# Triangle product and gated pair layer: four edits around the start and the end of the first stage

## The chip, the cores and the metric

The kernel runs on one core of one Trainium2 chip. The metric is the device time of one execution in microseconds (us). Three executions of the kernel before took 3205.04, 3205.08 and 3206.83 us; the median is 3205.08 us.

## What is computed

The input `x` is 384 x 384 positions of 128 channels in float32. Two layers follow each other.

```
z_n = layernorm(x)
a   = (z_n Wa + ba) * sigmoid(z_n Wga + bga)
b   = (z_n Wb + bb) * sigmoid(z_n Wgb + bgb)
t   = einsum('ijd,jkd->ikd', a, b)             # for each channel d one 384x384x384 product
x1  = x + (layernorm(t) Wo + bo) * sigmoid(z_n Wgo + bgo)

left  = x1 W_left + x1 W_eq + biases,  right = x1 W_right + b_right
out   = (left * sum_j right) * sigmoid(x1 W_gate + b_gate)
y     = layernorm(out W_out + b_out + x1)
```

## The kernel before

The work has three stages, and all of the change lies in the first and at its border to the second.

**Stage 1, projections.** The positions are cut into 72 tiles `n` (128 rows by 16 columns, `NT = 72`), and each tile into four steps `s = 4n + t` of four columns. A step (`step`, line 284) makes four products of 128x512 on TensorE (`proj` for `ga`, `a`, `gb`, `b`, line 305), two sigmoids on ScalarE (line 313), and on VectorE the two products `at` (line 326) and `bt` (line 342). `gate_project` (line 261) makes the eight small products `pgo` of the output gate (line 268) and adds their bias on VectorE into `gs` (line 270); `gate` (line 251) takes the sigmoid of `gs` on ScalarE into the tile `gt` (line 255), and after the fourth step of a tile stores `gt` to the DRAM tensor `G` from the GpSimd queue (line 258).

For tiles 0 to 2 `x` is normalised on ScalarE (line 222) and turned by TensorE. From tile 3 on (`OLD = 3`) a turned copy of `x` is loaded as `zT`. Its rows have to be multiplied by a factor per position: GpSimd makes the factors (`turned_factors`, lines 178 to 184, the last one a power), ScalarE copies them sixteen times into `again` (`repeat`, line 192, in the second step of the tile before), and `normalise_turned(s)` (line 196) multiplies. It is called in step `s - 2`. VectorE spreads the factors of two columns into the SBUF tile `every` and of the other two into the PSUM tile `pevery` (both line 210), and then GpSimd multiplies the first half and VectorE the second (both line 214). GpSimd also adds a bias to every tile for the residual (`residual`, line 233) and issues the stores of `Z` (234), `A` (330) and `G` (258).

The statistics of `x` (`bn_stats`, line 157, and `bn_aggr`, line 159) run on VectorE at the head of each step for columns that come some steps later. In step 0 they are those of the first four columns of tile 1, and the four GpSimd instructions of `norm_factors(1, 0, 4)` (lines 167 to 170) follow them.

The last 16 steps (`s >= S2 = 272`, tiles 68 to 71, the last group of 64 columns) leave out `gate_project`. Their 64 `pgo` products are made after the last step, in a row, "late gates": `gs`, sigmoid, store. `gt` comes from a pool of two buffers (`p1g`), `zT` from one of four (`p1z`), `gs` from one of three; the products of the projections share six PSUM banks.

**Stage 2, one 384x384x384 product per channel.** `fetch(d)` (line 640) loads the two factors of the `d`-th channel in the order of work, `ab_d`, from the DRAM tensors `A` and `B`, on SyncE's queue. Eight pairs are held. The pairs lie where pools of stage 1 lay: channels 0 to 3 mostly over a buffer of `bt`, channels 4 and 5 over buffers of `xt`. Channels under `BY_THIRDS = 2` are loaded by thirds of the rows of the sum: first two thirds (`fetch(d, 0, NB - 1)`), later the last third (`fetch(d, NB - 1)`), each third of `B` by a DMA of its own in pieces of 64 numbers (256 bytes). The other channels are loaded whole, in pieces of 768 bytes of `B`. The last rows and columns of `B` are still in SBUF (`b_held`) when stage 1 ends; `store_held` (line 661) stores them in pieces of some channels, of which the first covers channels 0 to 7. `multiply` (line 674) makes the products `pm` (line 679) in five PSUM banks: for `EARLY`, five (channel, row block) pairs of channels 0 and 1, first over two thirds, so that they don't need the last rows. `product` (line 685) ends them. VectorE subtracts channel 0 (`xd`, line 692), ScalarE squares (697), GpSimd adds (699), SyncE stores `X` (700).

**Stage 3** normalises, makes the second layer and stores; the change does not touch it.

The order on each engine is the order of the program. On SyncE's queue each DMA also waits until the one eight places before it has landed.

Of the kernel before, what the change touches and what calls it, by code (L numbers as in the profile page):

```python
# [9 lines left out]
FP = mybir.dt.float32  # L10
AF = mybir.ActivationFunctionType
ALU = mybir.AluOpType
# [8 lines left out]
def kernel(ctx: ExitStack, tc: tile.TileContext, ins, out: bass.AP):  # L21
# [15 lines left out]
    nc = tc.nc  # L37
    ctx.enter_context(tc.manual_schedule())
    P = 128
    x, xT = ins["x"][0], ins["xT"]  # L40
    N, C = x.shape[1], x.shape[2]
# [60 lines left out]
    CX, CT, BR = 16, 4, 32  # L102
    TS, TG = CX // CT, CG // CX
    OLD, SQ = 3, 32
    NT = NB * (N // CX)
    S2 = (NT - TG) * TS
# [4 lines left out]
    with tc.tile_pool(name="wprep", bufs=6) as wp, tc.tile_pool(name="p1s", bufs=3) as ps, tc.tile_pool(  # L111
        name="p1g", bufs=2
    ) as pgt, tc.tile_pool(name="p1z", bufs=4) as pz, tc.tile_pool(name="p1a", bufs=2) as pa_, tc.tile_pool(
        name="p1x", bufs=3
    ) as px, tc.tile_pool(name="p1b", bufs=1, side="right") as pb_, tc.tile_pool(name="p1t", bufs=2, space=PSUM) as ppt, tc.tile_pool(
        name="p1p", bufs=6, space=PSUM
    ) as ppp:
        tiles, turned, bts, gated, b_out_of = {}, {}, {}, {}, []
# [5 lines left out]
        def fetch(n):  # L124
            for _ in fetch_parts(n, 1):
                pass
# [27 lines left out]
        def statistics(first, last):  # L154
            for k in range(first, min(last, NT * CX)):
                n, c = divmod(k, CX)
                nc.vector.bn_stats(tiles[n]["st"][:, c, :], tiles[n]["x"][:, c, :])
                if n < OLD:
                    nc.vector.bn_aggr(tiles[n]["mv"][:, c, :], tiles[n]["st"][:, c, :])

        def norm_factors(n, c0=0, c1=CX, beside=nc.gpsimd):
            if n >= NT:
                return
            if n >= OLD:
                return turned_factors(n, c0, c1)
            mv, rstd, off = (tiles[n][k][:, c0:c1] for k in ("mv", "rstd", "off"))
            beside.tensor_scalar(rstd, mv[:, :, 1], EPS, None, ALU.add)
            beside.tensor_scalar(off, mv[:, :, 0], -1.0, None, ALU.mult)
            nc.gpsimd.tensor_tensor(rstd, rstd, mhalf[:, 0 : c1 - c0], ALU.pow)
            nc.gpsimd.tensor_tensor(off, off, rstd, ALU.mult)  # L170
            if c0 == 0:
                tiles[n]["zT"] = pz.tile([P, CX, C], FP, tag="zT", name=f"zn_{n}")
# [23 lines left out]
        def normalise_turned(s):  # L196
            n, t = divmod(s, TS)
            if n >= NT:
                return
            z = tiles[n]["zT"][:, t * CT : (t + 1) * CT, :]  # L200
            H = CT // 2
            for k, engine in enumerate((nc.gpsimd, nc.vector)):

                if k == 0:
                    every = ps.tile([P, H, P], FP, tag="every", name=f"every_{s}")
                else:
                    every = ppt.tile([P, CT, P], FP, tag="ptr", name=f"pevery_{s}")[:, 0:H, :]
                half = slice(k * H, (k + 1) * H)
                blocks = tiles[n]["again"][:, t * CT : (t + 1) * CT, :][:, half, :].rearrange("p c b -> p (c b)")
                nc.vector.transpose(  # L210
                    every.rearrange("p c (b r) -> p (c b) r", r=SQ),
                    blocks[:, :, None].to_broadcast([P, H * P // SQ, SQ]),
                )
                engine.tensor_tensor(z[:, half, :], every, z[:, half, :], ALU.mult)  # L214
            turned[s] = z

        def normalise(n, t, cs=range(CT)):
# [43 lines left out]
        def gate_project(s):  # L261
            n, t = divmod(s, TS)
            if t == 0:
                tiles[n]["gt"] = pgt.tile([P, CX, C], FP, tag="gt", name=f"gt_{n}")
            zT = turned[s]
            pgo = ppp.tile([P, CT, C], FP, tag="pk", name=f"pgo_{s}")
            for c in range(CT):
                nc.tensor.matmul(pgo[:, c, :], lhsT=zT[:, c, :], rhs=wT["go"], start=True, stop=True)  # L268
            gs = ps.tile([P, CT, C], FP, tag="gs", name=f"gs_{s}")
            nc.vector.tensor_tensor(gs, pgo, over(gate_bias, CT), ALU.add)  # L270
            gated[s] = gs
# [3 lines left out]
        FIRST_FACTORS = {  # L275
            0: ((1, 0, 4),), 1: ((1, 4, 8),), 2: ((1, 8, 12),), 3: ((1, 12, 16),),
            4: ((2, 0, 4),), 5: ((2, 4, 12),), 6: ((2, 12, 16),), 7: ((3, 0, 8),), 9: ((3, 8, 16),),
        }
        FIRST_RESIDUALS, FIRST_FETCHES = {2: 0, 5: 1, 9: 2, 10: 3}, {2: 3, 5: 4, 9: 5}

        def columns_ahead(s):
            return CX + CT * s + 2 * min(max(s - TS, 0), 2 * TS)

        def step(s):
            n, t = divmod(s, TS)
            r0, c0 = place(n)
            if t == 0:
                if n >= OLD:
                    fetch(n + 3)
                fetch_turned(n + 2)  # L290
                if s >= CATCH_UP:
                    norm_factors(n + 1)
                tiles[n]["at"] = pa_.tile([P, CX, P], FP, tag="at", name=f"at_{n}")
                if c0 % CG == 0:
                    bts[n // TG] = (pb_ if (NT - 1 - n) // TG % 2 else pb_held).tile(
                        [P, P, CG], FP, tag="bt", name=f"bt_{n}"
                    )
            at, bt = tiles[n]["at"], bts[n // TG]
            k0 = c0 % CG + t * CT
            zT = turned[s]  # L300
            ahead = (n + 1, t - 1) if t else (n, TS - 1)

            def proj(k):
                pk = ppp.tile([P, CT, P], FP, tag="pk", name=f"p{k}_{s}")
                nc.tensor.matmul(pk, lhsT=wT[k], rhs=zT, start=True, stop=True)  # L305
                return pk

            def by_rows(p):
                return p.rearrange("d c r -> d r c")

            def sigmoid(k, pg, by_row=False):
                sg = ps.tile([P, P, CT] if by_row else [P, CT, P], FP, tag="sg", name=f"sg{k}_{s}")
                nc.scalar.activation(sg, by_rows(pg) if by_row else pg, AF.Sigmoid, bias=bcol["g" + k])  # L313
                return sg

            statistics(columns_ahead(s), columns_ahead(s + 1))
            for factors in FIRST_FACTORS.get(s, ()):
                norm_factors(*factors)
            pga, pa = proj("ga"), proj("a")
            if s == 0:  # L320
                nc.tensor.matmul(biases[:, 1, :], lhsT=nb_w, rhs=raw["go"], start=True, stop=True)
                nc.vector.tensor_tensor(gate_bias, biases[:, 1, :], gate_bias, ALU.add)
            sga = sigmoid("a", pga)
            if 0 < s <= S2:
                gate(s - 1)
            nc.vector.scalar_tensor_tensor(
                at[:, t * CT : (t + 1) * CT, :], pa, bcol["a"], sga, ALU.add, ALU.mult
            )
            if t == TS - 1:
                nc.gpsimd.dma_start(out=A[:, c0 : c0 + CX, r0 : r0 + P], in_=at)  # L330
            pgb = proj("gb")
            sgb = sigmoid("b", pgb, by_row=True)
            if t == 1 and n + 1 >= OLD:
                repeat(n + 1)
            if s + 1 < OLD * TS:
                turn(s + 1)
                turned_out(s + 1)
            if s == 0:
                normalise(0, 2)
            normalise(*ahead)  # L340
            pb = proj("b")
            nc.vector.scalar_tensor_tensor(
                bt[:, :, k0 : k0 + CT], by_rows(pb), bcol["b"], sgb, ALU.add, ALU.mult
            )
            if s < S2:
                gate_project(s)
            if s + 2 >= OLD * TS:
                normalise_turned(s + 2)
            if s < CATCH_UP:
                if s in FIRST_RESIDUALS:  # L350
                    residual(FIRST_RESIDUALS[s])
                if s in FIRST_FETCHES:
                    fetch(FIRST_FETCHES[s])
            elif t == 1:
                residual(n + 1)
            if k0 + CT == CG and n < NT - 1:
                b_out_of.extend((bt, r0, c0 + CX - CG, k) for k in range(0, P, BR))
            if t == TS - 1 and b_out_of:
                bt, r0, k0, r = b_out_of.pop(0)
                nc.sync.dma_start(out=B[:, k0 // CG, r0 + r : r0 + r + BR, :], in_=bt[:, r : r + BR, :])  # L360
# [118 lines left out]
    x0, s1, s2, rs0 = (acc[:, k] for k in range(4))  # L479
    nc.gpsimd.memset(s1, 0.0)  # L480
    nc.gpsimd.memset(s2, 0.0)
    LAST, AHEAD, BY_THIRDS, R, HELD = 8, 6, 2, 4, 16
    group = {}

    def load(u):
# [135 lines left out]
    with tc.tile_pool(name="p2", bufs=1, side="right", reuse_waits="tile") as p2, tc.tile_pool(  # L621
        name="p2s", bufs=12, side="right", reuse_waits="tile"
    ) as p2s, tc.tile_pool(name="p2p", bufs=5, space=PSUM, reuse_waits="tile") as pp2, tc.tile_pool(
        name="p2q", bufs=2, space=PSUM, reuse_waits="tile"
    ) as pq2, tc.tile_pool(name="p2t", bufs=1, space=PSUM, reuse_waits="tile") as pt2:
        factors, products, squares = {}, {}, []
# [80 lines left out]
        for d in range(BY_THIRDS):  # L707
            fetch(d, NB - 1)
        store_held()
        for d in range(BY_THIRDS, AHEAD):  # L710
            fetch(d)
        store_held()
        for d, ib in EARLY:
            multiply(d, ib, range(NB - 1))
# [33 lines left out]
    with tc.tile_pool(name="p3s", bufs=4, reuse_waits="tile") as ps, tc.tile_pool(  # L748
        name="p3g", bufs=4, reuse_waits="tile"
    ) as pg3, tc.tile_pool(name="p3f", bufs=2, space=PSUM, reuse_waits="tile") as pfp, tc.tile_pool(  # L750
        name="p3y", bufs=2, space=PSUM, reuse_waits="tile"
# [294 lines left out]
```

## Time and profile before

| | |
|---|---|
| median of three executions | 3205.08 us |
| the profiled execution | 3205.72 us |
| its span, first to last instruction | 3203.9 us |
| TensorE busy | 3168.4 us, 99% |
| VectorE busy | 2703.2 us, 84% |
| GpSimd busy | 2414.4 us, 75% |
| ScalarE busy | 2009.0 us, 63% |
| stage 1 | 0 to 1283 us |
| stage 2 | 1283 to about 2045 us |

In the profile PE is TensorE, PEld its weight loads, DVE VectorE, ACT ScalarE, POOL GpSimd, SP SyncE. A row of the timeline gives the start in us from the span's start, the length, the engine, the line, what is written from what, and, in square brackets, how long the engine stood idle before it and what ended that.

### The profile page before, as it was taken

The page shows a single profiled execution, that of the slowest core. Times are in us where ns is not written, and L with a number is a line of the kernel's source. Part 1 is how long each engine was busy: PE and PEld are TensorE (multiplying, and loading weights), DVE is VectorE, ACT ScalarE, POOL GpSimd, SP SyncE. Part 2 cuts the span into 40 slices and gives each one's busy share as a digit, 9 for nine tenths or more (in the row PEclk, how much of TensorE's full clock was granted, in tenths as well). Part 3 has the DMA queues.
Part 4 walks back from the last instruction along what each step waited for, and adds up shares of the span by engine and source line. Part 5 has one row for each costly group of instructions (what it writes and reads, how often), then busy time and mean ns, then how long its engine had stood idle before and what let it go on. Part 6 is the DMA issues. An engine that isn't in the chain of part 4 may idle for free.

```text
span 3203.9 us, 51462 instructions
## 1 busy us (share of the span) xinstructions
PE 3168.4 (99%) x14543; PEld 2086.5 (65%) x14543; DVE 2703.2 (84%) x8313; ACT 2009.0 (63%) x5225; POOL 2414.4 (75%) x2113
## 2 busy tenths in 40 slices
PE   8999999999999999999999999999999999999998
PEld 5555555555555555555555555788888888888886
DVE  6999999999999997455555555999999999999999
ACT  7566666666666665222222222588888888888888
POOL 6788888888888876455555555499999998888888
PEclk9999999999999999999999999999999999999999
DMA  6989999999999998999999999777777777777774
GB/s 211 367 338 362 370 371 366 360 365 350 373 370 363 369 364 287 373 317 312 311 315 309 311 310 291 248 273 255 262 273 257 261 273 254 265 264 260 265 266 158
DMA packets 419195, 982.76 MB, mean 307 GB/s; under 512 B 30288, under 2 KB 326352, under 8 KB 373728
## 3 DMA queue, kind: packets, MB, share of 16 engines
q1 hardware_dynamic: 377984, 752.64, 67.5%
q0 software_dynamic: 40352, 226.57, 18.0%
q8 instruction: 118, 1.93, 0.2%
q14 instruction: 165, 1.35, 0.1%
q10 hardware_dynamic: 576, 0.26, 0.0%
HBM read 526.39 MB, written 452.98 MB: 306 GB/s over the span
## 4 chain that ended last, share of the span: by engine, by line
PE 95%; DMA 2%; POOL 1%; ACT 1%; issue 1%; DVE 1%; SPq 0%; ACTq 0%; POOLq 0%; DVEq 0%
PE pm L679 23%; PE py L519 8%; PE pf L789 8%; PE pleft L815 8%; PE pg L817 8%; PE pgo L268 7%; PE pga L305 7%; PE pa L305 7%; PE pgb L305 7%; PE pb L305 7%; PE ptr L542 4%; DMA B<-bt 1%; PE pg L828 0%; POOL acc L233 0%; DMA xt<-in_x_dram 0%
## 5 line engine op out<-in xcount | busy, mean ns | idle before, releaser
L679 PE MATMUL pm<-ab 128*128 128x384 f32 x2304 | 744.2, 486 | 2.0 <-DVE gs L270 2.0
L699 POOL TENSOR_TENSOR acc<-acc,xd 128x384 f32<-128x384 f32 x381 | 379.9, 997 | 361.9 <-DVE xd L692 361.8
L679 PEld LDWEIGHTS pm<-ab 128*128 128x128 f32 x2304 | 437.2, 190 | 306.4 <-DVE gs L270 2.6
L697 ACT ACTIVATE sq<-xd 128x384 f32<-128x384 f32 x381 | 188.4, 495 | 541.4 <-DVE xd L692 541.2
L692 DVE TENSOR_TENSOR xd<-pm,acc 128x384 f32<-128x384 f32 x381 | 212.3, 557 | 342.3 <-POOL acc L699 314.6
L807 ACT ACTIVATE res<-res,off,rs 128x128 f32<-128x128 f32 x1134 | 474.8, 485 | 0.4
L525 DVE SCALAR_TENSOR_TENSOR py<-py,acc,gr 128x128 f32<-128x128 f32 x1152 | 452.9, 393 | 0.9 <-PE py L519 0.2
L313 ACT ACTIVATE sga<-pga,c_L_conv_bga 128x512 f32<-128x512 f32 x288 | 197.9, 687 | 347.3 <-PE pga L305 345.6
L530 DVE BATCH_NORM_STATS2 st<-res 128x6 f32<-128x128 f32 x1128 | 375.3, 333 | 0.0
L268 PEld LDWEIGHTS pgo<-wT_go,xT 128*128 128x128 f32 x2208 | 287.5, 192 | 124.8 <-issue 78.4
L840 POOL TENSOR_TENSOR res<-res,r_L_conv_ln_bias 128x1536 f32<-128x1536 f32 (+1 forms) x96 | 326.5, 3401 | 7.5
L839 POOL TENSOR_TENSOR res<-res,r_L_conv_ln_scale 128x1536 f32<-128x1536 f32 (+1 forms) x96 | 326.9, 3406 | 0.6 <-ACT res L807 0.5
L233 POOL TENSOR_TENSOR acc<-xt,r_L_conv_b_out 128x2048 f32<-128x2048 f32 x72 | 327.0, 4541 | 0.0
L519 PE MATMUL py<-w_o,xr 128*128 128x128 f32 x2304 | 320.0, 275 | 0.0
L822 ACT ACTIVATE sg<-pg,c_L_conv_b_gate 128x384 f32<-128x384 f32 x384 | 223.2, 581 | 152.5 <-PE pg L817 103.6
L789 PE MATMUL pf<-w_o,h 128*128 128x128 f32 x2280 | 316.7, 275 | 0.0
L214 POOL TENSOR_TENSOR xT<-every,xT 128x256 f32<-128x256 f32 x276 | 202.0, 732 | 150.1 <-DVE every L210 144.4
L815 PE MATMUL pleft<-pairT,m_L_conv_W_left 128*128 128x384 f32 x768 | 311.6, 487 | 0.4 <-ACT pairT L543 0.4
L817 PE MATMUL pg<-pairT,m_L_conv_W_gate 128*128 128x384 f32 x768 | 310.6, 486 | 0.0
L305 PE MATMUL pga<-xT,wT_ga 128*128 128x512 f32 x552 | 284.1, 596 | 6.7 <-POOL xT L214 6.5
L519 PEld LDWEIGHTS py<-w_o,xr 128*128 128x128 f32 x2304 | 288.3, 192 | 0.8
L268 PE MATMUL pgo<-wT_go,xT 128*128 128x128 f32 x2208 | 288.5, 275 | 0.0
(187 smaller groups left out, 6667.6 us busy)
## 6 DMA issues: line engine op xcount, KB each, us to landing
Z<-acc POOLq DMA_DIRECT2D x72, 1024.0 KB, 10.5
A<-at POOLq DMA_DIRECT2D x72, 1024.0 KB, 13.4
G<-gt POOLq DMA_DIRECT2D x72, 1024.0 KB, 10.8
gr<-G SPq DMA_DIRECT2D x96, 768.0 KB, 5.7
zr<-Z SPq DMA_DIRECT2D x96, 768.0 KB, 7.2
xr<-X SPq DMA_DIRECT2D x96, 768.0 KB, 8.2
X<-xd SPq DMA_DIRECT2D x381, 192.0 KB, 5.6
xt<-in_x_dram SPq DMA_DIRECT2D x71, 1024.0 KB, 7.3
```

Source lines behind the costliest of these rows:

```text
L233: nc.gpsimd.tensor_tensor(zb, tiles[n]["x"], over(b_out, CX), ALU.add)
L268: nc.tensor.matmul(pgo[:, c, :], lhsT=zT[:, c, :], rhs=wT["go"], start=True, stop=True)
L305: nc.tensor.matmul(pk, lhsT=wT[k], rhs=zT, start=True, stop=True)
L519: nc.tensor.matmul(py[:, q, :], lhsT=g["x"][:, i, q * P : (q + 1) * P], rhs=w_o0, start=True, stop=True)
L525: nc.vector.scalar_tensor_tensor(py[:, q, :], py[:, q, :], rs0[:, q, u : u + 1], g["g"][:, i, q, :], ALU.mult, ALU.mult)
L530: nc.vector.bn_stats(b["st"][:, k, q, :], b["res"][:, k, q, :])
L679: nc.tensor.matmul(products[d, ib].rearrange("p (s c) -> p s c", c=CG), lhsT=ab[:, 0, q, ib * P : (ib + 1) * P], rhs=b_of(d)[:, :, q, :], ...
L699: nc.gpsimd.tensor_tensor(s1[:, ib, :], s1[:, ib, :], xd, ALU.add)
L789: nc.tensor.matmul(pf[:, q, :], lhsT=h[:, q * P : (q + 1) * P], rhs=w_o, start=True, stop=True)
L807: nc.scalar.activation(g["res"][:, i, q, :], g["res"][:, i, q, :], AF.Identity, bias=g["off"][:, i, q : q + 1], scale=g["rs"][:, i, q : q ...
L815: nc.tensor.matmul(pleft, lhsT=w_left, rhs=pairT, start=True, stop=True)
L817: nc.tensor.matmul(pg[:, 0:N], lhsT=w_gate, rhs=pairT, start=True, stop=True)
```

## The change

Four edits, with no change to the arithmetic:

1. For the last 16 steps `normalise_turned` makes one spread of 128x512 into PSUM and one product of 128x512, both on VectorE, in place of two spreads of 128x256, one product on GpSimd and one on VectorE.
2. For the same steps `gt` is not a tile of its own: the sigmoid of the late gates is written over the `zT` it was made from, and the store to `G` reads that.
3. In step 0 the statistics of tile 1 and the factors from them come after `gate_project`, not at the head of the step.
4. `BY_THIRDS` goes from 2 to 6: channels 2 to 5 are loaded by thirds as well, their first two thirds before the first `store_held` and their last third before the second one.

```diff
-            H = CT // 2
-            for k, engine in enumerate((nc.gpsimd, nc.vector)):
-                if k == 0:
+            H = CT // 2 if s < S2 else 0
+            for engine, k0, k1 in ((nc.gpsimd, 0, H), (nc.vector, H, CT)):
+                if k0 == k1:
+                    continue
+                if k0 < H:
                     every = ps.tile([P, H, P], FP, tag="every", name=f"every_{s}")
                 else:
-                    every = ppt.tile([P, CT, P], FP, tag="ptr", name=f"pevery_{s}")[:, 0:H, :]
+                    every = ppt.tile([P, CT, P], FP, tag="ptr", name=f"pevery_{s}")[:, k0:k1, :]
...
-                engine.tensor_tensor(z[:, half, :], every, z[:, half, :], ALU.mult)
+                engine.tensor_tensor(z[:, k0:k1, :], every, z[:, k0:k1, :], ALU.mult)
...
-                tiles[n]["gt"] = pgt.tile([P, CX, C], FP, tag="gt", name=f"gt_{n}")
+                tiles[n]["gt"] = tiles[n]["zT"] if s >= S2 else pgt.tile([P, CX, C], FP, tag="gt", name=f"gt_{n}")
...
-            statistics(columns_ahead(s), columns_ahead(s + 1))
-            for factors in FIRST_FACTORS.get(s, ()):
-                norm_factors(*factors)
+            def statistics_ahead():
+                statistics(columns_ahead(s), columns_ahead(s + 1))
+                for factors in FIRST_FACTORS.get(s, ()):
+                    norm_factors(*factors)
+
+            if s:
+                statistics_ahead()
...
             if s < S2:
                 gate_project(s)
+            if s == 0:
+                statistics_ahead()
...
-    LAST, AHEAD, BY_THIRDS, R, HELD = 8, 6, 2, 4, 16
+    LAST, AHEAD, BY_THIRDS, R, HELD = 8, 6, 6, 4, 16
...
         for d in range(BY_THIRDS):
             fetch(d, NB - 1)
         store_held()
-        for d in range(BY_THIRDS, AHEAD):
-            fetch(d)
         store_held()
```

More of the change, by code (lines that the diff above doesn't have):

```diff
@@ L200, in normalise_turned @@
             z = tiles[n]["zT"][:, t * CT : (t + 1) * CT, :]
-            H = CT // 2
-            for k, engine in enumerate((nc.gpsimd, nc.vector)):
-                if k == 0:
+            H = CT // 2 if s < S2 else 0
[3 more added lines that the diff above has]
+                if k0 < H:
                     every = ps.tile([P, H, P], FP, tag="every", name=f"every_{s}")
                 else:
-                    every = ppt.tile([P, CT, P], FP, tag="ptr", name=f"pevery_{s}")[:, 0:H, :]
-                half = slice(k * H, (k + 1) * H)
-                blocks = tiles[n]["again"][:, t * CT : (t + 1) * CT, :][:, half, :].rearrange("p c b -> p (c b)")
+                    every = ppt.tile([P, CT, P], FP, tag="ptr", name=f"pevery_{s}")[:, k0:k1, :]
+                blocks = tiles[n]["again"][:, t * CT : (t + 1) * CT, :][:, k0:k1, :].rearrange("p c b -> p (c b)")
                 nc.vector.transpose(
                     every.rearrange("p c (b r) -> p (c b) r", r=SQ),
-                    blocks[:, :, None].to_broadcast([P, H * P // SQ, SQ]),
+                    blocks[:, :, None].to_broadcast([P, (k1 - k0) * P // SQ, SQ]),
                 )
-                engine.tensor_tensor(z[:, half, :], every, z[:, half, :], ALU.mult)
+                engine.tensor_tensor(z[:, k0:k1, :], every, z[:, k0:k1, :], ALU.mult)
             turned[s] = z
```

## The prediction

> **What bounds the kernel now.** First the page's head and the waits of TensorE.
>
> ```profile
> span 3203.9 us, 51462 instructions
> PE 3168.4 (99%) x14543; PEld 2086.5 (65%) x14543; DVE 2703.2 (84%) x8313; ACT 2009.0 (63%) x5225; POOL 2414.4 (75%) x2113
> ```
>
> TensorE bounds it: all its idle time is 3203.9 - 3168.4 = 35.5 us, and the edits can win only from that. So I looked up who ends its waits.
>
> ```profile
> PE pga L305 <- POOL xT L214: 6.5, 8, 1.3
> PE pga L305 <- ACT zn L248: 4.0, 1, 4.0
> PE pm L679 <- DVE gs L270: 2.0, 1, 2.0
> PE pga L305 <- DVE r_L_conv_bgo L322: 1.7, 1, 1.7
> ```
>
> Three of these are the places of edits 1 (first row), 2 (third) and 3 (fourth). The timeline of the first step:
>
> ```profile
> 14.34 1.05 PE L268 MATMUL pgo<-wT_go,zn 128*128 128x128 f32 x8
> 14.35 3.19 ACT L222 ACTIVATE zn<-xt,off,rstd 128x128 f32<-128x128 f32 x8
> 15.06 0.29 DVE L157 BATCH_NORM_STATS2 st<-xt 128x6 f32<-128x128 f32 x1 [3.85 <-DMA xt<-in_x_dram]
> ...
> 16.67 0.28 DVE L322 TENSOR_TENSOR r_L_conv_bgo<-biases,r_L_conv_bgo 128x128 f32<-128x128 f32 x1
> ...
> 17.10 1.10 PE L305 MATMUL pga<-zn,wT_ga 128*128 128x512 f32 x2 [1.71 <-DVE r_L_conv_bgo L322]
> ```
>
> VectorE waits for tile 1 of x at the head of its queue, and L322, which frees the PSUM bank of the next pga, stands behind. TensorE's timeline at the end of stage 1, then GpSimd's and ScalarE's there:
>
> ```profile
> 1216.95 1.12 PE L305 MATMUL pga<-xT,wT_ga 128*128 128x512 f32 x2 [1.03 <-POOL xT L214]
> ...
> 1254.93 1.12 PE L305 MATMUL pga<-xT,wT_ga 128*128 128x512 f32 x2 [0.83 <-POOL xT L214]
> ...
> 1286.49 13.89 PE L679 MATMUL pm<-ab 128*128 128x384 f32 x42 [1.98 <-DVE gs L270]
> ```
>
> ```profile
> 1212.57 2.94 POOL L184 TENSOR_TENSOR rstd<-rstd,mhalf 128x16 f32<-128x16 f32 x1
> 1215.48 0.65 POOL L258 DMA_DIRECT2D G<-gt  x1
> 1216.15 0.74 POOL L214 TENSOR_TENSOR xT<-every,xT 128x256 f32<-128x256 f32 x1
> ```
>
> ```profile
> 1281.33 2.19 ACT L255 ACTIVATE gt<-gs 128x512 f32<-128x512 f32 x4 [3.79 <-DMA G<-gt]
> ```
>
> **Edit 3, step 0.** The moved statistics are eight VectorE instructions (15.06 to 16.67) and four GpSimd ones (L167 to L170, 1.81 us), no DMA; they are moved past L322, at, bt and gs. L322 can then run near 12.7, and pga follows pgo at TensorE's own pace (8 small products, 0.89 us): 14.34 + 0.89 = 15.23 instead of 17.10, **1.9 us**. What is late next? gs of step 0 ends near 16.1, tile 1 landed at 15.04, so the statistics end near 17.7 (1.1 later than now) and the factors at 19.5. ScalarE asks for them only after its row of eight (ends 17.54), two sigmoids, a gate and a copy: 19.8. That copy feeds the pga of step 2 at 15.23 + 4.76 = 19.99; 0.1 us to spare. After that each early step costs TensorE 4.76 us, ScalarE 4.1 and VectorE less, so both catch up. Later idle times (4.0 at 61.98, 1.5 at 147, three for L214) follow from chains of engines that start from these steps and should move along; from 180 to 1208 TensorE has no gap. Bounds: 0 (given back at the 4.0 us wait) to 2.0.
>
> [...] After the 4.0 us gap two products take 1.91 and 1.77 instead of 1.02 (starts 1.71 and 1.60 apart, not 0.86: 1.6 us), and the granted clock of the stretch 60 to 80 is 0.91. From the row, a gap that only moves costs the same 1.6. [...] I take 0 and widen the range.
>
> **Edit 1, last 16 steps.** A step is 4 x 0.858 = 3.43 us of TensorE; 16 are 54.9, and they take 1268.76 - 1208.79 = 59.97. So 5.0 us are gaps, one per two steps, nearly all for GpSimd: its 0.73 us product (16 of them, removed) stands behind the power (2.94), a DMA issue (0.65) or the residual (4.53). On VectorE the work of a step changes from 0.36 + 0.45 + 0.34 (starts apart) to one spread and one product of 128x512. The spread has no row at that size: 0.36 for 256 and about 0.27 for 256 more and 0.09 for PSUM, 0.72 (at most 2 x 0.45 = 0.90). The product is of the shape of L270, 0.60. Sum 1.32, +0.17. With statistics (0.78), at (0.65) and bt (0.66) a step is 3.41 against TensorE's 3.43: VectorE just fits, until step 279; then it has no statistics and 0.8 to spare.
>
> What is late next is ScalarE: L192, 3.63 us once a tile, delays the sigmoid, so at, bt and then the spread for two steps on. I lay this out by rows. Tile 69: L192 ends 1219.31, at 1220.06, bt done 1221.4, spread and product 1222.8; TensorE, no longer stopped at 1216.95, could start step 276 at 1222.63 and starts at 1222.9 (now 1224.13). Tile 70: L192 ends 1233.8, so at, bt, 1.32: step 280 at 1237.35 (now 1239.52), 0.6 late. at of step 280 waits for the store of A issued near 1224, which now lands at 1241.9; that may cost 0.4 at step 282. Tile 71: step 284 at 1251.75 (now 1254.93), and 4 x 3.43 + 0.1 later 1265.6 instead of 1268.76. **3.1 us.** Bounds: 5.0 if all gaps go; if the spread takes 0.90 and the product 0.69, VectorE's step is 3.68, 8 steps lose 0.25 each and each tile the 1.35 us for which VectorE now waits for L192: about 0.5 left.
>
> **Edit 2, late gates.** ScalarE waits 3.79 us for the third gt until a store of G landed (7.2 us); gs has three buffers, so VectorE stops, and the last gs (1286.43) holds the PSUM bank of the second pm. Without it the gates follow the pgo (0.89 each) and gs ends 0.7 us after the last pgo, while six products (6 x 0.323 = 1.9 us) can run: the whole 1.98 goes, **2.0 us**. The added wait: the built program shows that the first xd now waits for the last store of G (its memory was zT). With TensorE at P = 1279.9 (1283.06 - 3.1), that store is issued near P + 2 and lands 7 to 10 us later (the four now: 7.0, 7.2, 8.9, 10.0): P + 9 to P + 12; xd is wanted at P + 9.3. Behind it on VectorE stand all other xd and squares, behind these GpSimd's sums and SyncE's X stores. TensorE needs that bank only for the third pm of channel 2, 48 products on: P + 15.5. Three us to spare, so 0; a landing after 17 us (one store of A took 17.5) would cost 4.
>
> **Edit 4, loads by thirds.** Twelve more DMAs. In the packet records 256 bytes take 18 ns, 768 take 36, 1536 take 65, 4608 take 178. So on 16 engines a channel by thirds costs 3 x 768 x 18/16 = 2.59 us for B and 1.56 for A, whole 1.73 and 1.42: +1.0, four channels +4.0 us of DMA. Two thirds of it fall into this hole (us, busy times, clock, DMA share, GB/s):
>
> ```profile
> 1260.00:1264.00 4.00, 4.00 (x10) 1.71 (x9) 3.06 (x8) 1.58 (x3) 1.29 (x2) 1.00 0.27 80
> 1264.00:1268.00 4.00, 4.00 (x11) 1.80 (x10) 2.16 (x4) 1.37 (x2) 0.08 (x1) 1.00 0.02 4
> ```
>
> [...] By rule or row the sum is 0, as nothing waits: channel 2 is wanted at P + 11.6 = 1291.5, and loaded whole as now (B issued 1283.2, landing up to 13.6 later) it could be up to 5 late once TensorE is 5 us earlier. So edit 4 wins nothing itself but keeps edits 1 and 2 from ending in a load. On SyncE's queue the 12 new issues stand before the first store_held (1266.6) and should be through by 1264. **0**, bounds 0 to 3.
>
> **Sum.** 3205.72 (profiled; span 3203.9 and 1.8 around it) - 1.9 - 3.1 - 2.0 = 3198.7; the median lies 0.6 lower, so **3198.1**, 0.22% faster. About 0.2% (6.4 us, 3198.7) is what a measurement of this kernel can tell from no change.
>
> **Rivals.**
> - A: VectorE and L192 take GpSimd's place. For it: 3.41 of 3.43 us and an estimated spread. Against: statistics end at step 279. Edit 1 wins 1.3: 3199.9. Chance 0.18.
> - B: the 1.9 us of the start is given back at the 4.0 us wait. For: ScalarE has 0.1 to spare. Against: that wait hangs on statistics of step 9, no DMA. 3200.0. Chance 0.08.
> - C: better: half-rate period missed, 1.6 more: 3196.3. Chance 0.07.
> - D, slower: SyncE's queue. Each DMA waits for the one eight before it. At the landings seen at 1242 (8.4 us, 1.05 per DMA) twelve take 12.6; at 13 us they take 20, and store_held (7.5 to land) and channel 0's last third (4.7 to 7.6) come at 1286.5, just when wanted (P + 6.5). From there each us counts. At 26 us, as one store of B took, they take 39: 15 us lost, 3213. Against: the hole. Chance 0.05.
> - Likeliest: 3197.0 to 3199.6, 0.62, of which 0.41 below 3198.7.
>
> Faster 0.41 + 0.07 = 0.48; same 0.21 + 0.18 + 0.08 = 0.47; slower 0.05. The range 3196.4 to 3201.6 leaves out D, half of C and some of the ends.
>
> **What would show it.** pga of step 1 starts at 15.2, and the sum of gaps before 180 falls by 1.9. No wait for POOL in the last 16 steps, gaps of 0.3 to 0.6 at steps 276, 280, 284 ended by VectorE, VectorE's spread of 0.7. No gap between pgo and pm; xd waits for G 0 to 3 us. DMA share above 0.5 at 1260 to 1268. A wait of pm for a load, or a store of G that lands over 13 us after its issue, would make it wrong.

## The result and the profile after

Sixteen executions of the changed kernel have a median of 3199.11 us (3198.70 to 3200.36), sixteen of the kernel before, on the same chip, 3206.47 us (3205.01 to 3207.55). The ratio is 0.9979, with a 95% interval of 0.9972 to 0.9985: 7.4 us or 0.2% faster. The forecast was 3198.1 us, from 3196.4 to 3201.6: 7.0 us under 3205.08, the median of three executions of the kernel before. The sixteen lie 1.4 us above those three, so 7.4 us were won and the median is still 1.0 above the forecast. The profiled execution took 3198.70 us against 3205.72, 7.0 us less, as the sum had it. So the total came out; the experiments show that the 2.0 us of edit 2 would have come without it.

The head of the page of the changed kernel, and the waits of TensorE in its trace (us in total, times, longest; lines 308, 216, 250 and 333 are 305, 214, 248 and 326 of before):

```profile
span 3196.9 us, 51440 instructions
PE 3166.8 (99%) x14543; PEld 2087.0 (65%) x14543; DVE 2705.2 (85%) x8297; ACT 2008.9 (63%) x5225; POOL 2402.4 (75%) x2097
```

```profile
PE pga L308 <- ACT zn L250: 4.0, 1, 4.0
PE pga L308 <- POOL xT L216: 3.2, 3, 1.3
PE pgb L308 <- DVE at L333: 1.5, 1, 1.5
...
PE pga L308 <- issue: 0.8, 1, 0.8
...
PE pga L308 <- DVE xT L216: 0.6, 1, 0.6
```

Idle time of TensorE is 3196.9 - 3166.8 = 30.1 us, 5.4 less; the other 1.6 us of the 7.0 lie in time that the profile counts as busy. The wait for the gate bias in step 0 and the one before the first `pm` are gone, GpSimd's product ends three waits instead of eight, and two short ones are new, 0.6 for VectorE's product and 0.8 with no releaser. The first row, 4.0 us, was there before and has stayed; it will matter. The timeline of step 0, and TensorE's at the end of stage 1:

```profile
12.39 0.29 DVE L329 TENSOR_TENSOR r_L_conv_bgo<-biases,r_L_conv_bgo 128x128 f32<-128x128 f32 x1 [1.35 <-PE biases L328]
...
14.35 1.05 PE L271 MATMUL pgo<-wT_go,zn 128*128 128x128 f32 x8
...
15.24 1.02 PE L308 MATMUL pga<-zn,wT_ga 128*128 128x512 f32 x2
```

```profile
1206.63 1.02 PE L308 MATMUL pga<-xT,wT_ga 128*128 128x512 f32 x2
...
1235.32 1.13 PE L308 MATMUL pga<-xT,wT_ga 128*128 128x512 f32 x2 [0.64 <-DVE xT L216]
...
1250.12 1.10 PE L308 MATMUL pga<-xT,wT_ga 128*128 128x512 f32 x2 [0.80 <-issue]
...
1263.93 14.45 PE L271 MATMUL pgo<-wT_go,xT 128*128 128x128 f32 x128
1278.22 22.10 PE L689 MATMUL pm<-ab 128*128 128x384 f32 x68
```

The same places in the kernel before:

```profile
1208.79 1.12 PE L305 MATMUL pga<-xT,wT_ga 128*128 128x512 f32 x2
...
1268.76 14.45 PE L268 MATMUL pgo<-wT_go,xT 128*128 128x128 f32 x128
1283.06 1.46 PE L679 MATMUL pm<-ab 128*128 128x384 f32 x4
```

The first projection of step 1 follows the small products at once (15.24, was 17.10). Steps 272 to 287 take 1263.93 - 1206.63 = 57.30 us, were 1268.76 - 1208.79 = 59.97. The first `pm` follows the last `pgo`, and no gap comes behind it: the third product starts 4 x 0.323 = 1.29 us after the first, was 1286.49 - 1283.06 = 3.43. Step 272 itself starts 1208.79 - 1206.63 = 2.16 us sooner. So the trace divides the 7.0 us into 2.16 at the start, 2.67 in the sixteen steps and 2.14 at the border. The hole in the transfers is filled (each row: the stretch, its length, busy us and number of instructions of PE, PEld, DVE, ACT and POOL, TensorE's granted clock with 1.00 for full speed, share of the DMA engines, GB/s):

```profile
1260.00:1264.00 4.00, 4.00 (x11) 1.78 (x10) 1.60 (x3) 1.90 (x3) 0.47 (x1) 1.00 1.23 273
1264.00:1268.00 4.00, 4.00 (x38) 4.00 (x37) 3.05 (x5) 1.73 (x3) 0.69 (x1) 1.00 1.15 304
```

Its share was 0.27 and 0.02. The loads by thirds do take the time that was free.

### The profile page after: what moved, and what is told of

Same layout as the page of the kernel before. It is cut to its first block, busy times and chain, and to the rows that moved or that the text cites. A ratio compares the mean times of both kernels' runs of the same rounds, so it can differ in the third digit from the quotient of the medians.

```text
span 3196.9 us, 51440 instructions
## 1 busy us (share of the span) xinstructions
PE 3166.8 (99%) x14543; PEld 2087.0 (65%) x14543; DVE 2705.2 (85%) x8297; ACT 2008.9 (63%) x5225; POOL 2402.4 (75%) x2097
## 4 chain that ended last, share of the span: by engine, by line
PE 96%; POOL 1%; ACT 1%; DVE 1%; issue 1%; DMA 0%; ACTq 0%; POOLq 0%; DVEq 0%
PE pm L689 23%; PE py L529 8%; PE pf L797 8%; PE pleft L823 8%; PE pg L825 8%; PE pgo L271 8%; PE pga L308 7%; PE pgb L308 7%; PE pa L308 7%; PE pb L308 7%; PE ptr L552 4%; PE pg L836 0%; POOL rstd L184 0%; POOL acc L235 0%; ACT res L815 0%
## 5 line engine op out<-in xcount | busy, mean ns | idle before, releaser
L535 DVE SCALAR_TENSOR_TENSOR py<-py,acc,gr 128x128 f32<-128x128 f32 x1152 | 384.1, 333 | 0.9
L540 DVE BATCH_NORM_STATS2 st<-res 128x6 f32<-128x128 f32 x1128 | 306.7, 272 | 0.0
L216 POOL TENSOR_TENSOR xT<-every,xT 128x256 f32<-128x256 f32 x260 | 190.2, 732 | 141.5 <-DVE every L212 136.0
```

Of the source, the lines that this page charges most:

```text
L535: nc.vector.scalar_tensor_tensor(py[:, q, :], py[:, q, :], rs0[:, q, u : u + 1], g["g"][:, i, q, :], ALU.mult, ALU.mult)
```

## The experiments

My theory was the sum of the prediction: three gains that add, and an edit 4 that wins nothing by itself. The rivals: the start gives its gain back at the 4.0 us wait; the repeats and VectorE set the last steps; the thirds are the real gain. The experiments ran in three groups, each on one chip; the median of the kernel before was 3206.5, 3206.7 and 3206.6 us beside them. The changed kernel was timed in the first comparison alone, so a difference to it can be off by some 0.2 us. Each kernel ran 13 to 21 times, the four with the repeats after the copy on the changed kernel only five times each.

| kernel | median us | single times | ratio to before, 95% interval |
|---|---|---|---|
| changed | 3199.11 | 3198.70 to 3200.36 | 0.9979 (0.9972 to 0.9985) |
| changed without edit 3 | 3201.17 | 3200.28 to 3203.51 | 0.9983 (0.9976 to 0.9989) |
| changed without edit 1 | 3201.66 | 3201.21 to 3202.83 | 0.9986 (0.9979 to 0.9992) |
| changed without edit 2 | 3199.61 | 3198.97 to 3200.65 | 0.9980 (0.9972 to 0.9987) |
| changed without edit 4 | 3205.16 | 3201.89 to 3207.44 | 0.9995 (0.9987 to 1.0003) |
| before with edit 4 only | 3207.64 | 3206.30 to 3209.12 | 1.0002 (0.9994 to 1.0010) |
| changed without edits 1 and 2 | 3205.89 | 3204.17 to 3207.57 | 0.9997 (0.9989 to 1.0006) |
| changed, repeats after the copy | 3193.42 | 3193.34 to 3193.47 | 0.9959 (0.9945 to 0.9973) |
| changed, late factors and repeats early | 3202.55 | 3202.20 to 3203.83 | 0.9989 (0.9982 to 0.9995) |
| repeats after the copy, later weights | 3191.95 | 3191.91 to 3192.21 | 0.9955 (0.9942 to 0.9967) |
| repeats after the copy, four by thirds | 3193.29 | 3193.21 to 3193.53 | 0.9959 (0.9945 to 0.9972) |
| before, repeats after the copy | 3201.25 | 3199.70 to 3203.90 | 0.9984 (0.9977 to 0.9990) |
| repeats after the copy, factors early | 3193.00 | 3192.84 to 3193.16 | 0.9958 (0.9945 to 0.9970) |

**Edit 3 taken back.**

```diff
-            if s:
-                statistics_ahead()
+            statistics_ahead()
...
-            if s == 0:
-                statistics_ahead()
```

> The changed kernel with step 0's statistics back at the head of the step, all else as changed. My theory: the start was worth what the shift of the later gaps shows, 1.9 us, and 0.2 us more because the stretch at half clock then fell on slightly cheaper work; so 2.1 us slower than the changed kernel, with the first projection of step 1 at 17.1 us instead of 15.24 and the gap before step 10 at 65.9 instead of 63.99. Rival (the start's gain is given back at the 4.0 us wait for the turned copy before step 10): within 0.5 us of the changed kernel, with that wait shorter by the same amount. Second rival: the clock stretch moves and the whole differs from 2 us by up to 1.7 us either way.

Measured: 3201.17, 2.06 us slower. TensorE's rows at step 1 and step 10:

```profile
16.38 1.10 PE L308 MATMUL pga<-zn,wT_ga 128*128 128x512 f32 x2 [1.15 <-DVE r_L_conv_bgo L328]
```

```profile
65.22 2.07 PE L308 MATMUL pga<-zn,wT_ga 128*128 128x512 f32 x2 [3.97 <-ACT zn L250]
67.09 1.91 PE L308 MATMUL pa<-zn,wT_a 128*128 128x512 f32 x2
68.80 1.91 PE L308 MATMUL pgb<-zn,wT_gb 128*128 128x512 f32 x2
```

The wait before step 10 is as long as in the changed kernel (3.95), so the first rival (given back) falls. In this profiled execution tile 1 landed at 14.3 us, not at 15.04 as in the profile of before, and the first projection of step 1 came at 16.38. So the wait that edit 3 takes away is as long as the load is late: 1.1 us here, 1.9 there. The second rival (the clock) is in this trace too: behind the wait the granted clock was halved for 6.8 us (0.50 in the stretch from 64 to 68 and 0.65 in the one to 72, 2.0 + 1.4 us of full clock missing, twice that is the length), in the changed kernel for 3.4. TensorE is 1.2 us later than in the changed kernel at step 10 and 2.5 at step 11. So the 2.06 us of the medians hold both, and how much of it is the wait alone is not shown.

**Edit 1 taken back.**

```diff
-            H = CT // 2 if s < S2 else 0
+            H = CT // 2
```

> The changed kernel with the halves on GpSimd and VectorE in all steps, also the last sixteen. My theory: from step 272's first projection to the gates takes 60.0 us as before the change instead of 57.3, so 2.7 us slower than the changed kernel, with waits of TensorE on GpSimd's product of 1 to 2.5 us at steps 276, 280 and 284. Rival (the ScalarE repeats and not the products are what is late): 1 us or less slower, with the waits of 0.6 and 0.8 us at steps 280 and 284 still there and GpSimd hardly in them.

Measured: 3201.66, 2.55 us slower, with nine waits for GpSimd's product again (in the changed kernel 3.2 us, three times):

```profile
PE pga L308 <- POOL xT L216: 6.7, 9, 1.3
```

From step 272 to the gates it takes 1266.59 - 1206.62 = 59.97 us, as before. The theory's size holds; its waits of 1 to 2.5 us at three steps are five of 0.3 to 1.0. The rival (1 us) falls.

**Edit 2 taken back.**

```diff
-                tiles[n]["gt"] = tiles[n]["zT"] if s >= S2 else pgt.tile([P, CX, C], FP, tag="gt", name=f"gt_{n}")
+                tiles[n]["gt"] = pgt.tile([P, CX, C], FP, tag="gt", name=f"gt_{n}")
```

> The changed kernel with the late gates written into a tile of their own again. My theory: a gap of 2.0 us comes back between the last gate product and the first product of the two matrices, and the first differences no longer wait for the last gate store; 2.0 us slower. Rival (the wait for the gate store that the shared tile brings costs TensorE something a little later): the gap comes back but the whole is less than 1 us slower.

Measured: 3199.61, only 0.5 us slower, and no gap. Neither the theory nor the rival had that. The rows of ScalarE, VectorE and TensorE at the border:

```profile
1277.47 2.19 ACT L257 ACTIVATE gt<-gs 128x512 f32<-128x512 f32 x4 [3.61 <-DMA G<-gt]
```

```profile
1281.68 0.69 DVE L273 TENSOR_TENSOR gs<-pgo,r_L_conv_bgo 128x512 f32<-128x512 f32 x1 [1.06 <-ACT gt L257]
```

```profile
1279.38 20.81 PE L689 MATMUL pm<-ab 128*128 128x384 f32 x64
```

The gates do wait 3.61 us for a store again, and the last `gs` ends at 1282.37, 3.0 us after the products began; and TensorE runs through. The semaphores of the built programs say why. In the kernel before, and in each kernel here without edit 1, the third product of stage 2 waits for the last `gs`; in the kernels with edit 1 the seventh does: another order of the PSUM banks. A product of 128x384 shows as two records, 0.323 us apart. Had the third waited here, TensorE would have stood from 1279.38 + 4 x 0.323 = 1280.67 to 1282.37; the seventh is due at 1279.38 + 12 x 0.323 = 1283.3, and by then the bank is free. So edit 1 removes the gap also without edit 2. Why the banks turn with edit 1 I did not follow up. The 0.5 us are no clock stretch: both kernels' times fall into two groups about 1.1 us apart, and this kernel's lie 0.4 higher in each. In the traces 0.5 us lie behind the first `pm` (1919.2 us to the end of the span, 1918.7 in the changed kernel), 0.4 of them behind TensorE's last product; why is open.

**Edits 1 and 2 taken back.** Both diffs above.

> The changed kernel without edit 1 and without edit 2: halves on two engines to the end, and the late gates in a tile of their own. Each of the two was seen to remove the 1.98 us gap by itself: edit 2 because the gates no longer wait for a store, edit 1 because it moves the last gate bias's bank from the third product of the next stage to the seventh. Theory: without both the gap is back, so 2.6 us (edit 1's steps) and 2.0 us (the gap) and at most 0.5 more: 4.6 to 5.1 us slower than the changed kernel. Rival (the two edits simply add, each with the size that its own removal showed): 2.6 + 0.5 = 3.1 us slower, and no gap.

Measured: 3205.89, 6.8 us slower, more than both said. The gap is back, and longer (2.72 us, 1.98 in the kernel before; what lengthened it was not tested):

```profile
1280.91 1.46 PE L689 MATMUL pm<-ab 128*128 128x384 f32 x4
1285.09 60.33 PE L689 MATMUL pm<-ab 128*128 128x384 f32 x181 [2.72 <-DVE gs L273]
```

```profile
1286.00:1288.00 2.00, 2.00 (x4) 1.01 (x3) 0.00 (x0) 0.00 (x0) 1.43 (x2) 0.50 1.03 319
```

Behind the gap the granted clock was 0.88, 0.50 and 0.77 in three stretches of 2 us from 1284 on: (0.12 + 0.50 + 0.23) x 2 = 1.7 us of work lost. So 2.7 for the steps, 1285.09 - 1280.91 - 1.29 = 2.9 for the gap and 1.7 for the clock make 7.3; this profiled execution was 7.7 us longer than that of the changed kernel (0.4 come later), the median 6.8. The theory and the rival had left out the clock. Beside edit 1, edit 2 is worth 0.5 us; without it, 3205.89 - 3201.66 = 4.2.

**Edit 4 taken back.**

```diff
-    LAST, AHEAD, BY_THIRDS, R, HELD = 8, 6, 6, 4, 16
+    LAST, AHEAD, BY_THIRDS, R, HELD = 8, 6, 2, 4, 16
...
         store_held()
+        for d in range(BY_THIRDS, AHEAD):
+            fetch(d)
         store_held()
```

> The changed kernel with only two channels loaded by thirds and the four others whole after the held store, as before the change. My theory, with the loads of channels 2 to 5 held until the last A store has landed: channel 2 lands 0 to 5 us after TensorE wants it, since TensorE now comes to it 2 us sooner after the gates than before; I put it at 2.5 us slower. Rival (the whole loads are in time, and the hole in the transfers was free either way): within 0.5 us of the changed kernel, with no wait of TensorE for the matrices of channel 2.

Measured: 3205.16, 6.1 us slower, more than twice the 2.5 expected and nearly all that the change wins. TensorE's timeline, and the stretches from 1294 on with the clock in the third column from the end:

```profile
1278.14 11.78 PE L689 MATMUL pm<-ab 128*128 128x384 f32 x36
1293.75 6.46 PE L689 MATMUL pm<-ab 128*128 128x384 f32 x11 [3.83 <-DMA ab<-B]
```

```profile
1294.00:1298.00 4.00, 4.00 (x7) 2.18 (x8) 0.91 (x3) 0.49 (x1) 1.82 (x2) 0.50 1.06 357
1298.00:1302.00 4.00, 4.00 (x12) 2.20 (x12) 2.01 (x4) 0.99 (x2) 1.72 (x2) 0.86 1.06 361
```

36 records are the 18 products of channels 0 and 1. Then TensorE waits 3.83 us for the whole load of `B` of channel 2, issued at 1278.06 and landing 15.6 us later, since behind the last A store all loads run together (DMA share 1.0). When it goes on the clock is at half (0.66 from 1292 to 1293, 0.50 from there): 0.125 from 1293.75 to 1294, 2.0 and 0.56 us of work lost, 2.7 in all. 3.8 + 2.7 = 6.5, and the span is 6.5 longer.

**Edit 4 alone, on the kernel before.** The last diff the other way round.

> The kernel before with six channels by thirds as its only edit. In the run with two by thirds TensorE waited 3.83 us for channel 2 and then ran a stretch at half clock, 6.6 us in all; in the kernel before, the same whole load of channel 2 landed about 0.1 us ahead of TensorE, whose 1.98 us wait for the last gate bias just covered it. Theory: alone the edit is worth nothing, because the wait for the bias stays and nothing else was late: 0.5 us faster to 0.5 us slower than the kernel before. Rival (the kernel before lost time to channel 2 too, in the executions that were not profiled): 1 to 3 us faster. Second rival (4 us more of transfer work is paid somewhere): 1 to 4 us slower.

Measured: 3207.64 beside 3206.68; the interval spans 1, from 1.9 us faster to 3.2 slower, so a small cost of the thirds is not excluded. The kernel before did not lose by channel 2 in its trace: the load, issued at 1283.18 and landing up to 13.6 later, came by 1296.8, and TensorE, held 1.98 us by the bias, asked at 1286.49 + 32 x 0.323 = 1296.8. The bias wait is still there in this kernel (2.39 us in its trace).

**The 4.0 us wait, and the clock.** The wait that edit 3 could only move is ScalarE's: the sixteen repeats of tile 3 stand before the turned copy that step 10 needs.

```diff
-            if t == 1 and n + 1 >= OLD:
+            if t == 1 and n + 1 > OLD:
                 repeat(n + 1)
             if s + 1 < OLD * TS:
                 turn(s + 1)
                 turned_out(s + 1)
+            if n + 1 == OLD and t in (1, 2):
+                repeat(OLD, 2 * (t - 1), 2 * t)
```

> The changed kernel, with the sixteen ScalarE repeats of tile 3 behind the turned copy of their step, and in two lots of eight in steps 9 and 10, so that the copy for step 10 does not wait for them. Theory: the 3.95 us wait before step 10 goes, and with it the stretch at half clock that comes 0.1 to 3.5 us behind it: 3.9 + 1.7 to 2.1 = 5.6 to 6.0 us faster than the changed kernel. Rival on the clock (the stretch at half clock is not set off by this wait, and falls on other work): 3.9 us faster. Rival on the wait (another engine was as late): under 2 us faster.

Measured: 3193.42, 5.7 us faster than the changed kernel. The stretch from 60 to 68 in the changed kernel, and then in this one:

```profile
60.00:64.00 4.00, 0.05 (x2) 0.01 (x1) 1.86 (x8) 3.76 (x16) 4.00 (x1) 0.96 0.03 10
64.00:68.00 4.00, 4.00 (x6) 1.84 (x7) 0.40 (x1) 1.21 (x2) 0.78 (x2) 0.61 0.70 174
```

```profile
60.00:64.00 4.00, 4.00 (x16) 2.04 (x15) 2.70 (x9) 3.87 (x13) 4.00 (x1) 1.00 0.03 12
64.00:68.00 4.00, 4.00 (x17) 2.25 (x16) 3.57 (x11) 3.36 (x11) 2.54 (x4) 1.00 0.69 162
```

The wait is gone and so is the half clock, (0.04 + 0.39) x 4 = 1.7 us: 3.95 + 1.7 = 5.65. The traces have TensorE that much sooner behind step 10, and 0.3 goes back at the next wait for GpSimd's product, here first in the changed kernel and then in this one:

```profile
79.81 1.13 PE L308 MATMUL pga<-xT,wT_ga 128*128 128x512 f32 x2 [0.61 <-POOL xT L216]
```

```profile
74.48 1.12 PE L308 MATMUL pga<-xT,wT_ga 128*128 128x512 f32 x2 [0.93 <-POOL xT L216]
```

So the two profiled executions differ by 5.2 us; the medians differ by more because the changed kernel's other executions are longer than its profiled one. Both rivals fall. And the five single times lie within 0.13 us of each other, the changed kernel's sixteen within 1.7.

**The same on the kernel before.**

> The kernel before, with only the repeats of tile 3 put behind the turned copy and split in two lots, without the four edits. Theory: the 3.95 us wait and its stretch at half clock go there as well: 5.6 to 6.0 us faster than the kernel before, 3200.6 to 3201.0. Rival (TensorE then comes sooner to the end of the first stage and gives part back at the loads of channel 2, which in the kernel before were just in time): only 2 to 4 us faster. The single times should lie closer together if the stretch at half clock, by where it falls, is what spreads them.

Measured: 3201.25, 5.3 us faster; between theory and rival. Its single times still spread over 4.2 us: its gap of 2.0 at the border remains, and in its trace the clock was 1.00 around it. So the gap of step 10 is not all that spreads the times of the kernel before. The late load of step 0 adds to it (the first projection of step 1 came at 16.66 here, at 17.10 in the profile of before); what the border adds I have only from the kernels in which it is covered.

**Late factors and repeats early.** In the last four tiles the factors are made before the A store of the step before, and the repeats come in a tile's first step.

```diff
-                if s >= CATCH_UP:
+                if CATCH_UP <= s < S2:
                     norm_factors(n + 1)
...
             if t == TS - 1:
+                if s >= S2 - 1:
+                    norm_factors(n + 2)
                 nc.gpsimd.dma_start(out=A[:, c0 : c0 + CX, r0 : r0 + P], in_=at)
...
-            if t == 1 and n + 1 >= OLD:
+            if t == (0 if s >= S2 else 1) and n + 1 >= OLD:
```

> The changed kernel, in whose last four tiles the factors are worked out ahead of the A store on GpSimd, a step sooner, and the ScalarE repeats follow in the first step of the tile instead of the second. Theory (the repeats, held by GpSimd's power and followed by VectorE's products, set the steps 276, 280 and 284): the waits of 0.3, 0.64 and 0.80 us go, 1.2 to 1.7 us faster than the changed kernel. Rival (VectorE's own 3.45 us for a step sets them): under 0.5 us faster, and the waits stay.

Measured: 3202.55, 3.4 us slower. The theory falls, and so does the rival, which had no loss. ScalarE's repeats of one tile, and GpSimd ahead of them:

```profile
1227.00 3.64 ACT L192 COPY again<-rstd 32x16 f32<-32x16 f32 x16 [1.85 <-POOL rstd L184]
```

```profile
1222.40 0.23 POOL L178 TENSOR_TENSOR off<-st 128x16 f32<-128x16 f32 x1 [4.31 <-DVE st L157]
```

The factors could not be made sooner: GpSimd waited for statistics, which VectorE had not made, and behind it the A store waited too. VectorE runs about a step behind TensorE here, and while there are statistics its 3.45 us a step (TensorE's is 3.43) do not let it catch up.

**The same with the repeats left in place, on the faster kernel.** The last diff without its last two lines.

> The kernel with the repeats behind the copy (3193.4 us), in which the factors of the last tiles are worked out ahead of the A store, with the ScalarE repeats left in the second step of a tile. The run that moved both lost 3.4 us: its repeats stood 1.85 us, because the factors waited for statistics that VectorE, a step behind TensorE, had not made. Theory: with the repeats a step later that wait is covered, the 0.48 us that they wait for GpSimd's power go, and 0.3 to 0.5 us is gained. Rival (VectorE's 3.45 us a step keeps it behind, so nothing that is made ready sooner helps): within 0.3 us of 3193.4, with the waits at steps 276, 280 and 284 still there.

Measured: 3193.00 against 3193.42 of the same kernel without it. 0.4 is within the theory's 0.3 to 0.5, but beside 3193.29 of the next kernel, which ran on the same chip, it is 0.3: the size is not settled. The trace settles the waits: those at steps 280 and 284 (0.66 and 0.81 us without this edit) are gone, against the rival, and one at step 282 is new and takes more than half of it back, which the theory did not have:

```profile
1237.36 1.13 PE L308 MATMUL pga<-xT,wT_ga 128*128 128x512 f32 x2 [0.83 <-DVE xT L216]
```

**Four channels by thirds.** `BY_THIRDS` 4 and the loop of whole fetches back, on the faster kernel.

> The kernel with the repeats behind the copy (3193.4 us), in which four channels are loaded by thirds and channels 4 and 5 whole after the held store. Theory (what counts is that the load of channel 2, and perhaps of 3, is begun in the hole of the transfers): within 0.3 us of 3193.4. Rival (the load has to be spread over all six, since a whole load takes 10 to 15.6 us when several are queued): channel 4 is wanted 11.6 us after channel 2 and comes late too, 2 to 6 us slower.

Measured: 3193.29, no wait for a load. It is enough to begin the loads of channels 2 and 3 in the hole; the rival falls.

**Later weights.**

```diff
-            if s >= 2 * CATCH_UP:
+            if s >= 2 * CATCH_UP + 2:
                 next(later, None)
```

> The kernel with the repeats behind the copy (3193.4 us), in which the preparation of the second layer's weights also begins two steps later, in step 26 instead of 24. In the trace a VectorE addition of 128 numbers, one to a partition, takes 4.48 us at 134.55, just as GpSimd's residual addition (134.40, 4.61 us) runs beside it, and TensorE waits 1.47 us at 140.5. Theory (the small addition stands still for as long as GpSimd's large one runs): two steps later it runs alone in about 0.1 to 0.2 us and the wait goes: 1.5 us faster than 3193.4, or 2.7 if the wait of 1.28 us at 153.7 is its echo. Rival (that addition waits for its data, not for GpSimd): no gain.

Measured: 3191.95, 1.5 us faster than without it (1.3 beside the kernel of four channels, on the same chip), and the best of all, 0.9955 of the kernel before. GpSimd's and VectorE's rows, first without and then with this edit:

```profile
134.40 4.61 POOL L235 TENSOR_TENSOR acc<-xt,r_L_conv_b_out 128x2048 f32<-128x2048 f32 x1
134.55 4.48 DVE L402 TENSOR_TENSOR c_L_conv_b_left<-c_L_conv_b_left,c_L_conv_b_eq 128x1 f32<-128x1 f32 x1
```

```profile
144.73 0.18 DVE L402 TENSOR_TENSOR c_L_conv_b_left<-c_L_conv_b_left,c_L_conv_b_eq 128x1 f32<-128x1 f32 x1
```

An addition of 128 numbers took 4.48 us beside GpSimd's addition and 0.18 away from it. TensorE's 1.47 us wait for `at` at 140.5 is gone; the one of 1.28 at 153.7 is not, it became 0.57 and 1.16.

## Why the prediction was right, step by step

- **Edit 3, 1.9 us: right for the two profiled executions.** 1.86 at the first projection, 2.16 at step 272. Nothing was given back (rival B). About 0.2 of the added 0.3 is the clock: behind the 4.0 us wait it was halved in both kernels, and less of it met work: 1.54 us of full clock missing behind the gap, 1.71 in the kernel before. The term had been taken as fixed, though; it is the lateness of one load, 1.1 us in another trace, and that the medians too show 2.06 is in part the clock.
- **The clock, taken as 0: right for the total, too small as a risk.** The dip did not vanish (rival C, whose sum should read 3198.1 - 1.6 = 3196.5). The 0 is the row's; by how much the range had to be widened beside it was the author's estimate, and no run shows that figure. What the traces show is a dip of two lengths. A stretch at half clock of 3.4 us: in the kernel before (0.89, 0.50, 0.50, 0.50 and 0.90 in the stretches of 1 us from 66 on, in all 1.71 us of full clock missing, twice that is the length) and in the changed kernel (0.83, 0.50, 0.50, 0.50 and 0.96 from 63 on, 1.71 again). And one of double that, 6.8 to 6.9 us: at step 10 in the kernel without edit 2 (0.56 and 0.58 in the two stretches of 4 us from 62 on) and in the one without edit 3, and at the wait for the load in the one without edit 4 (0.66, six times 0.50 and 0.92 from 1292 to 1300). These three lost 2.7 to 2.8 us of work behind the gap, over 1 us more than the row's 1.6. The kernel without edit 2 and the changed one stood 0.11 us apart at the end of the 4.0 us wait and 1.08 the other way 17 us on. The single times of the changed kernel lie in two groups 1.1 us apart (3198.7 to 3199.2 and 3199.6 to 3200.4), which one stretch of 3.4 us or one of 6.8 would give; that link is argued, not shown for each execution.
- **Edit 1, 3.1 us: right, 0.4 too high.** Measured 2.67 in the trace and 2.55 by taking it back. The spread is 0.71 to 0.72 long (reckoned 0.72), the product 0.61 from its start to the next (0.60); VectorE's step with statistics 3.45 (reckoned 3.41). Step 280 came at 1235.32, as reckoned (1237.35 less the 2.16 of the start is 1235.19), step 284 at 1250.12, 0.5 later than reckoned. The repeats waited 0.48 us for GpSimd's power and so held the sigmoid:

```profile
1242.81 3.64 ACT L192 COPY again<-rstd 32x16 f32<-32x16 f32 x16 [0.48 <-POOL rstd L184]
```

- **Edit 2, 2.0 us: the gap went, the attribution failed.** The step that failed is "the last gs (1286.43) holds the PSUM bank of the second pm". That was read from the kernel before; with edit 1 it is the fourth `pm` that needs that bank, and the gap went without edit 2, whose own worth beside edit 1 is 0.5 us. Where edit 1 is absent the step holds: the kernel without edit 1 has no gap, the one without both has. So two edits each close the same gap, and the sum put it down to one. The cover was mis-sized too: six products are 6 x 2 x 0.323 = 3.9 us, not 1.9. The added wait was there and free: `xd` started at 1289.19, 11.0 us behind the first `pm`, 1.6 later than in the kernel without edit 2, and TensorE did not notice.
- **Edit 4, 0 us and "keeps edits 1 and 2 from ending in a load": right, and the larger part of the story.** The text put channel 2 at "up to 5 late" without it; 3.83 was measured. What it missed is the 2.7 us of half clock behind such a wait. The prediction has its 0 "by rule or row": no run shows the rule, and what the runs show is that the 256-byte pieces cost nothing that can be told: without edit 4 the kernel is 6.1 us slower, with four channels by thirds it is the same (3193.29 against 3193.42), and alone on the kernel before the edit's +1.0 us cannot be told from 0.
- **Rival D** did not come: the twelve issues were through at 1264.2 and the held store went at 1264.98.

The three terms of the sum missed by +0.3, -0.4 and +0.1 in the profiled executions; that they cancel is luck. The edits do not add. In one order of adding them to the kernel before: edit 4 +1.0 (no difference that can be told), edit 3 -1.75, edit 2 -4.2, edit 1 -2.55. In another order the same edits would show other sizes: edit 2 last -0.5, edit 4 last -6.1.

## What to carry to other kernels

When a border between stages holds several near-equal waits (here a bank, a store and a load, within 4 us of each other), price the edits as a set, and reread from the changed program who waits for which bank: what a removed wait is worth is set by the wait behind it. Each of the nine TensorE gaps of 2.7 us or more whose clock was read (seven at step 10, 2.72 and 3.83 us at the border) had a stretch at 0.50 of the clock behind it; where it was read to its end, it cost 1.5 to 2.8 us more: count it with the gap. And look first at the longest wait in the list: moving sixteen small copies behind one urgent copy won 5.7 us more, three quarters of what the four edits won together.

## What the runs showed that I had not expected

- A gap of 2.72 us was followed by 3.4 us at half clock; one of 2.39 us in the trace of another kernel was not (1.00 in each stretch from 1280 to 1304). What makes the difference is not shown.
- With no gap of TensorE over 1.5 us after the start, single times lie within 0.13 to 0.32 us (five executions of each of four kernels); with the gap of 4.0, within 1.6 us or more (13 to 21 executions).
- Two additions, each of two SBUF tiles, on GpSimd and VectorE: VectorE's of 128 numbers took 4.48 us beside GpSimd's of 4.61 and ended with it (139.03 and 139.01), and took 0.18 away from it. What holds it these rows do not show.
